# Block one's last 1x1 convolution: half of its tiles made once behind the 3x3 stage and kept, the Gram matrix for the other half only

## The chip, the cores and the metric

The kernel runs on one core of one Trainium2 chip. The metric is device time in microseconds (us) of one execution: TensorE (PE in the profile) with its weight loads (PEld), VectorE (DVE), ScalarE (ACT), GpSimd (POOL), and the DMA engines, which are fed by queues on SyncE (SP), ACT and POOL. A tile framework puts the semaphores between the engines; each engine and each queue works through its own instructions in order. Where an instruction isn't pinned to the order of the program, a scheduler places it on its engine.

## The reference

Two residual blocks, one behind the other, in fp32, on x of 64 images, 1024 channels, 14 x 14 pixels:

```
out = relu(bn(conv(x,   w1, b1, 1, 0), g1, be1))     # 1x1, 1024 -> 256
out = relu(bn(conv(out, w2, b2, 1, 1), g2, be2))     # 3x3,  256 -> 256
out = bn(conv(out, w3, b3, 1, 0), g3, be3)           # 1x1,  256 -> 1024
out = softplus(residual_scale)[0] * out
out = relu(x + out)
```

`bn` takes mean and variance of each channel over all images and pixels (12544 of them) in the call itself. So no convolution's result can be normalized before the convolution has been made, or its statistics have been had in another way, for all images.

## The kernel before

Channels lie on the 128 partitions in slots: 1024 channels are 8 slots (`CS`), 256 are 2 (`MS`). The pixels are cut into T = 32 tiles of two images, 392 pixels (`PX`) each. A tile of x is 128 x 8 x 392 fp32, 1568 KB. The result of conv1 and conv2, `y_all`, stays on the chip; the result of block one, `mids`, goes to DRAM and comes back in block two. PSUM is handled by `Psum`, which gives out banks by tag (ax, ay, ap for conv1; cx, cy, cp for conv3).

The two 1x1 convolutions are made by a scheme of seven products in place of eight half-size ones (`Seven`, with `Conv1` and `Conv3`): sums of the weight blocks (`combine_w1`, `combine_w3`) and of the input blocks (`column_sums` for conv3) are made ahead, products p1 to p7 run on PE, and an `after1` to `after7` behind each product adds it to where it belongs. A conv3 unit makes two slots of output (q and q + 4) of a tile, from 7 matmuls of 196 columns; a tile has four units. A conv1 unit makes a whole tile, by 28 matmuls of 196 columns. `stream` puts the products of neighbouring units into the order in which they are issued.

In `Conv3`, ACT copies three of the products out with the scale of the normalization (line 352, called from `saved`), DVE adds the scaled others into the tile of x in place (line 519), POOL adds ACT's copies (lines 540 and 545), ACT applies shift and relu, and behind the tile's last unit ACT's queue stores the tile to `mids`.

Block one goes: conv1 of all tiles; the 3x3 stage `conv2`; the statistics of conv3; and the stage `fused`. The statistics of conv3's result are not taken from that result. `gram` makes the Gram matrix of conv3's input: y is normalized (ACT, `norm`), a constant is subtracted (DVE, line 1179), chunks of 128 pixels are turned so that pixels lie on partitions, and for each of the 98 chunks PE multiplies the chunk with itself (`cp<-zt` and `ap<-zt` in the profile; the PE array is used there as 128 x 64 tiles). The first pieces are turned by PE (line 1221), the others by pieces moved by DMA (line 1200, queues of SP and POOL) and turned by DVE in 32 x 32 blocks (line 1237). `conv3_stats` (lines 1317 to 1366) makes mean and variance of every output channel from it by a few matmuls with w3. Eight plain conv3 results of tile 0 (`made`) are issued around it, and `affine` turns statistics into scale and shift.

`fused` (line 1422) interleaves two streams one to one: conv3 of tiles 1 to 31 (`last_convs`) with conv1 of block two on tiles 0 to 31 (`first_convs`), the former LAG = 14 products ahead. A tile of x is loaded by SP one tile ahead of its use (`load_x`, one DMA), turns into a tile of block one's output in place, and is then the input of conv1. There are two pools of x tiles with two buffers each, used by even and odd tiles in turn. Block two ends with the same Gram stage and `final`.

Of the kernel before, what the change touches and what calls it, by code (L numbers as in the profile page):

```python
# [14 lines left out]
P = 128  # L43
# [21 lines left out]


# [24 lines left out]
def bottlenecks(ctx: ExitStack, tc: tile.TileContext, x, w1s, w2s, w3s, pars, out):  # L91
# [8 lines left out]
    mids = [dram.tile([P, CS * PX], FP, tag=f"mid{t}", name=f"mid{t}") for t in range(T)]  # L100
    us = [
# [45 lines left out]
    def sums_tile(pool, n):  # L147

        return pool.tile([P, n, 4 * CS // 2 * P], FP, tag="ws", name="ws")

    def combine(a, s):

        s = s.rearrange("p (i s m) -> p i s m", i=4, m=P)
        s = [s[:, i] for i in range(4)]
        def work():
            for to, one, op, two in (
                (s[0], a[1][0], ALU.add, a[1][1]), (s[1], s[0], ALU.subtract, a[0][0]),
                (s[2], a[0][0], ALU.subtract, a[1][0]), (s[3], a[0][1], ALU.subtract, s[1]),
            ):
                tc.keep_in_program_order(nc.vector.tensor_tensor(to, one, two, op))  # L160
                yield

        return (a, s), work()
# [4 lines left out]
    def combine_w3(w, s):  # L168
        n = CS // 2
        return combine([[w[:, k, o * n : (o + 1) * n] for k in range(MS)] for o in range(2)], s)  # L170
# [183 lines left out]
    class Conv1(Seven):  # L354
# [5 lines left out]
        def __init__(self, psum, pool, xs, ts, w1, par, stats, border):  # L360
            self.psum, self.pool, self.ts, self.par, self.stats = psum, pool, ts, par, stats
            self.border = border if ts[-1] == T - 1 else None
            self.pinned = ts[-1] >= T - 1 - len(ts)
# [64 lines left out]
        def result(self, o, i, bank, more=None):  # L428
# [11 lines left out]
            if len(self.ts) == 2 or o != i:  # L440

                self.run(nc.vector.bn_stats(self.stats[:, o, self.ts[i % len(self.ts)], :], whole), o, i)
# [32 lines left out]
    def column_sums(pool, ys, n, twice=(2, 3)):  # L475
# [6 lines left out]
        nc.vector.tensor_sub(t3, ys[1][1], ys[0][1])  # L482
        nc.vector.tensor_add(t2, t3, ys[0][0])
        nc.vector.tensor_sub(t1, ys[0][1], ys[0][0])
        nc.vector.tensor_sub(t4, ys[1][0], t2)
        return sums

    class Conv3(Seven):
# [6 lines left out]
        def __init__(self, psum, pool, xt, q, n, ys, sums, w3, aff, to):  # L495
# [5 lines left out]
            self.u12 = pool.tile([P, 2 * n], FP, tag="cu12", name="cu12", bufs=2)  # L501
# [48 lines left out]
        def end(self):  # L550
            for row in range(2):
                self.relu(row)
            if self.to is not None:
                nc.scalar.dma_start(out=self.to, in_=self.xt.rearrange("p s f -> p (s f)"))

# [576 lines left out]
    def gram(psum, pool, homes, aff, minus_c, beside):  # L1132

        upper, lower = psum.tile(3 * Q + 1, "cp"), psum.tile(2 * Q + 2, "ap")
        zts = [pool.tile([P, CH, M + 2], FP, tag=f"zt{i}", name=f"zt{i}") for i in range(NZT)]
# [4 lines left out]
        def ends(v):  # L1142

            (step, n), (_, _) = v.ap
            return bass.AP(v.tensor, v.offset + 1, [[step, n], [3 * Q, 2], [1, Q + 1]])
# [4 lines left out]
        once, twice = 1.0 / NPX, 2.0 / NPX  # L1150
# [3 lines left out]
        for i, here, cols, value in (  # L1154
# [6 lines left out]
            nc.gpsimd.memset(by[i][here, cols], value)  # L1161

# [71 lines left out]
        def by_vector(k, i):  # L1234
            zt, x = next(zts), home(k)[0].rearrange("p s j f -> p (s j) f")
            tc.keep_in_program_order(
                nc.vector.transpose(
                    zt[:, :, 1 : M + 1].rearrange("p b (n c) -> p b n c", c=32),
                    x[:, :, i * CH * 32 : (i + 1) * CH * 32].rearrange("p n (b r) -> p b n r", r=32),
                )  # L1240
            )
# [55 lines left out]
        for k, zt in enumerate(itertools.chain(pairs(), (None,))):  # L1297
            if before is not None:
                for c in range(CH):
                    first, last = k == 1 and c == 0, k == total and c == CH - 1  # L1300
                    v = before[:, c]
                    for q, with_ in enumerate((v[:, : 3 * Q + 1], v[:, Q + 1 :], v[:, 2 * Q + 1 :], ends(v))):
                        here = slice(q % 2 * Q, q % 2 * Q + Q)
                        to = (upper, lower)[q // 2][here]
                        to = to[:, : 2 * Q + 1] if q == 2 else to
                        if q == 3:
                            to = to.rearrange("p (k m) -> p k m", k=2)
                        matmul(
                            to, v[:, 1 + q * Q : 1 + q * Q + Q], with_, start=first, stop=last,
                            tile_position=(0, q % 2 * Q), skip_group_check=True,  # L1310
                        )
# [5 lines left out]
    def conv3_stats(psum, one, grams, w3, mv, tags, spare):  # L1317
# [10 lines left out]
        turned = psum.tile(P, "ax")  # L1328
# [6 lines left out]
        nc.scalar.activation(g0[high, 0:1], g0[high, M + 1 :], AF.Copy)  # L1335
        means = g0[:, 0:1], g1[:, M + 1 :]
        wide = 64
        sums = [psum.tile(CS * wide, tag).rearrange("p (o k) -> p o k", k=wide) for tag in ("ax", "ap")]
# [8 lines left out]
        for h in range(2):  # L1347
# [3 lines left out]
            matmul(t0, g0[:, left], w3[:, 0, cols, :], start=True, stop=True)  # L1351
            matmul(t1, g0[:, right], w3[:, 0, cols, :], start=True, stop=False)
            matmul(t1, g1[:, right], w3[:, 1, cols, :], start=False, stop=True)
            qs = [q[:, s, h * half * P : (h + 1) * half * P] for s in range(MS)]
            for s, t in ((0, t0), (1, t1)):
                nc.vector.tensor_mul(qs[s], t, w3[:, s, cols, :].rearrange("p o c -> p (o c)"))
            nc.vector.tensor_add(qs[0], qs[0], qs[1])
        for o in range(CS):
            matmul(sums[0][:, o], by_mean[:, o * P : (o + 1) * P], ones, start=True, stop=True)
        for o in range(CS):  # L1360
            matmul(sums[1][:, o], q[:, 0, o * P : (o + 1) * P], ones, start=True, stop=True)
        nc.vector.tensor_copy(mv[:, :, 0], sums[0][:, :, 0])
# [59 lines left out]
    def fused(psum, pool, xpools, xs, w1, w3, aff, par, stats, border, begun):  # L1422

        def last_convs():
            for t in range(1, T):
                if t + 1 < T:
                    xs.append(load_x(xpools[(t + 1) % 2], 0, t + 1))
                ys = [[two(t, s)[:, i * H // 2 : (i + 1) * H // 2] for i in range(2)] for s in range(MS)]  # L1430
                n = PX // 2
                sums = column_sums(pool, ys, n)
                for q in range(CS // 2):
                    yield Conv3(psum, pool, xs[t], q, n, ys, sums, w3, aff, mids[t] if q == CS // 2 - 1 else None)

        def first_convs():
            for t in range(T):
                yield Conv1(psum, pool, xs[t : t + 1], (t,), w1, par, stats, border)

        a, c = stream(first_convs(), T), stream(last_convs(), (T - 1) * CS // 2)  # L1440
# [5 lines left out]
        while True:  # L1446
            more = next(a, "end"), next(c, "end")
            if more == ("end", "end"):
                break

# [202 lines left out]
    for b in range(2):  # L1653
# [9 lines left out]
        with tc.tile_pool(name=f"last_{b}", bufs=1) as one, tc.tile_pool(  # L1663
# [4 lines left out]
            if b == 0:  # L1668
                w1 = load_w1(one, b + 1, nc.sync)
            aff = affine(aggregate(stats2, 0), pb, G2, BE2)  # L1670
            with ExitStack() as scope:
                if b == 0:
                    psum = Psum(scope, ["cy", "ay", "cx", "cy", "ay"], cy=2, ay=2)
                else:
                    psum = Psum(scope, ["cy", "cx"], cy=2, cx=2, cp=2)
                with tc.tile_pool(name=f"gram_{b}", bufs=1) as pool:
                    def x_tile(name, t=0):
                        return xpools[t].tile([P, CS * PX], FP, tag="x", name=name)


                    ws = sums_tile(one, 2 - b)
                    homes = [x_tile("home"), x_tile("home") if b else ws.rearrange("p i n -> p (i n)"), x_tile("home", 1)]

                    made_c, summed = combine_w3(w3, ws[:, 0])
                    weights = [made_c]
                    total = NPX // (CH * P)
                    if b == 0:
                        made_a, more = combine_w1(w1, ws[:, 1])
                        weights = [made_a, made_c]
                        beside = {total - 10: partial(list, summed), total - 4: partial(list, more)}  # L1690
                    else:
                        beside = {total - 14 + 2 * i: partial(next, summed) for i in range(4)}
                    grams = gram(psum, pool, homes, aff, minus_c, beside)

                    made = [conv3(psum, 0, 0, w3, "cx" if b else "ay")]
                    mv3 = small.tile([P, CS, nc.vector.BN_AGGR_DIM], FP, tag="mv3", name="mv3")
                    conv3_stats(psum, pool, grams, w3, mv3, ("cy", "cp", "cy", "cp" if b else "cx"), homes[2])
                made.append(conv3(psum, 0, 1, w3, "cx" if b else "ay"))
                tags = ("cy", "cp") * 2 if b else ("cy", "cx", "cy")
# [59 lines left out]
```

## Time and profile before

| | |
|---|---|
| median of the runs | 1913.37 us (1912.12 to 1913.9, 3 runs) |
| span of the profiled execution | 1910.9 us |
| from the span's start to the end of `conv2` | 0 to 584 us |
| Gram stage | 584 to 645 us |
| conv3's statistics, tile 0, start of `fused` | 645 to 671 us |
| `fused` | 671 to about 1254 us |
| last stage of block two, after its Gram stage | about 1610 to 1911 us |

The page gives the busy time of each engine, the chain of work that ended last, and groups of instructions by line, engine and tile name. A group's row has the count, the busy time, the mean length of one in ns, and the idle time of its engine before it with what ended that. An fp32 matmul shows as two records. The windows view gives, for each stretch, the busy time of every engine, the granted clock of TensorE (1.00 is full), the share of time in which the 16 DMA engines were busy and the bandwidth. The timeline merges neighbouring instructions of one group into one row: start, length, group, count.

### The profile page before, as it was taken

The page shows a single profiled execution, that of the slowest core. Times are in us where ns is not written, and L with a number is a line of the kernel's source. Part 1 is how long each engine was busy: PE and PEld are TensorE (multiplying, and loading weights), DVE is VectorE, ACT ScalarE, POOL GpSimd, SP SyncE. Part 2 cuts the span into 40 slices and gives each one's busy share as a digit, 9 for nine tenths or more (in the row PEclk, how much of TensorE's full clock was granted, in tenths as well). Part 3 has the DMA queues.
Part 4 walks back from the last instruction along what each step waited for, and adds up shares of the span by engine and source line. Part 5 has one row for each costly group of instructions (what it writes and reads, how often), then busy time and mean ns, then how long its engine had stood idle before and what let it go on. Part 6 is the DMA issues. An engine that isn't in the chain of part 4 may idle for free. (4 is left out here: it accounts for less than half of the span.)

```text
span 1910.9 us, 28713 instructions
## 1 busy us (share of the span) xinstructions
PE 1899.0 (99%) x10232; PEld 1594.9 (83%) x10232; DVE 1541.5 (81%) x2491; ACT 1085.6 (57%) x2160; POOL 581.6 (30%) x682
## 2 busy tenths in 40 slices
PE   9999999999999999999999999999999999999999
PEld 5555557999998799999999999989999987555555
DVE  5787767999998867776777777689999986888886
ACT  2222214677778355555555555557777782666665
POOL 0111100211204143333334333302121051666665
PEclk9999999999999999999999999999999999999999
DMA  7777644887856544444444444258779467799997
GB/s 288 273 248 271 219 166 144 208 224 213 215 171 172 190 158 176 170 169 169 174 185 176 175 169 169 111 191 216 217 206 226 143 166 274 263 349 334 354 342 274
DMA packets 198527, 408.77 MB, mean 214 GB/s; under 512 B 37104, under 2 KB 175024, under 8 KB 181872
## 3 DMA queue, kind: packets, MB, share of 16 engines
q1 hardware_dynamic: 159712, 321.85, 49.3%
q0 software_dynamic: 33056, 34.03, 8.6%
q10 hardware_dynamic: 5616, 51.06, 6.4%
q8 instruction: 81, 1.33, 0.3%
q14 instruction: 62, 0.51, 0.1%
HBM read 263.75 MB, written 115.34 MB: 198 GB/s over the span
## 5 line engine op out<-in xcount | busy, mean ns | idle before, releaser
L352 ACT ACTIVATE cu<-cy,scale 128x196 f32<-128x196 f32 (+1 forms) x552 | 256.2, 473 | 275.2 <-PE cy L179 272.6
L179 PE MATMUL columns<-v,ub 128*128 128x224 f32 (+1 forms) x1536 | 302.3, 338 | 1.1 <-ACT columns L352 0.8
L352 ACT ACTIVATE x<-x,shift 128x392 f32<-128x392 f32 x452 | 255.2, 613 | 73.1 <-POOL x L545 53.6
L179 PEld LDWEIGHTS columns<-v,ub 128*128 128x128 f32 x1536 | 268.8, 188 | 6.7 <-ACT columns L352 1.5
L519 DVE SCALAR_TENSOR_TENSOR x<-cp,scale,x 128x196 f32<-128x196 f32 (+1 forms) x368 | 178.1, 484 | 95.3 <-PE cp L179 94.1
L179 PE MATMUL cy<-ct,ws 128*128 128x196 f32 (+1 forms) x736 | 221.6, 383 | 0.7 <-ACT cu L352 0.7
L540 POOL TENSOR_TENSOR x<-x,cu 128x196 f32<-128x196 f32 (+1 forms) x184 | 165.6, 900 | 172.9 <-ACT cu L352 164.2
L179 PE MATMUL ay<-at,ws 128*128 128x196 f32 (+1 forms) x768 | 212.8, 382 | 0.0
L545 POOL TENSOR_TENSOR x<-x,cu 128x392 f32<-128x392 f32 x124 | 125.9, 1016 | 191.4 <-DVE x L519 191.4
L179 PEld LDWEIGHTS ay<-at,ws 128*128 128x128 f32 x768 | 139.3, 190 | 34.7 <-issue 0.2
L179 PEld LDWEIGHTS cy<-ct,ws 128*128 128x128 f32 x736 | 133.6, 190 | 35.3 <-ACT cu L352 2.6
L179 PE MATMUL l<-diffs,ub 128*128 128x224 f32 (+1 forms) x768 | 149.6, 337 | 0.3 <-ACT sd L1492 0.3
L567 POOL TENSOR_TENSOR x<-x,cu 128x392 f32<-128x392 f32 x120 | 125.5, 1047 | 73.2 <-DVE x L519 72.3
L179 PE MATMUL m<-sums,ua 128*128 128x224 f32 (+1 forms) x752 | 146.0, 336 | 0.2 <-DVE sums L683 0.2
L352 ACT ACTIVATE au<-ay 128x196 f32<-128x196 f32 (+1 forms) x140 | 53.4, 381 | 150.2 <-PE ay L179 142.7
L179 PEld LDWEIGHTS l<-diffs,ub 128*128 128x128 f32 x768 | 134.6, 189 | 1.2 <-ACT sd L1492 0.6
L519 DVE SCALAR_TENSOR_TENSOR x<-cx,scale,x 128x196 f32<-128x196 f32 (+1 forms) x184 | 88.9, 483 | 57.0 <-PE cx L179 57.0
L179 PEld LDWEIGHTS m<-sums,ua 128*128 128x128 f32 x752 | 131.5, 189 | 1.3 <-DVE sums L683 0.7
L179 PE MATMUL cy<-y,w 128*128 128x196 f32 (+1 forms) x408 | 125.1, 393 | 0.0
L179 PE MATMUL cx<-y,w 128*128 128x196 f32 (+1 forms) x400 | 122.7, 392 | 0.0
L179 PE MATMUL cp<-y,ws 128*128 128x196 f32 (+1 forms) x368 | 112.1, 386 | 0.0
L179 PE MATMUL cy<-ct,w 128*128 128x196 f32 (+1 forms) x368 | 111.1, 384 | 0.6 <-ACT cu L352 0.5
(237 smaller groups left out, 3903.7 us busy)
## 6 DMA issues: line engine op xcount, KB each, us to landing
x<-in_x SPq DMA_DIRECT2D x62, 1568.0 KB, 7.0
ub<-u SPq DMA_DIRECT2D x92, 768.0 KB, 5.6
x<-mid SPq DMA_DIRECT2D x32, 1568.0 KB, 8.8
mid<-x ACTq DMA_DIRECT2D x31, 1568.0 KB, 5.1
out<-x SPq DMA_DIRECT2D x123, 392.0 KB, 6.8
ua<-u SPq DMA_DIRECT2D x92, 256.0 KB, 3.1
u<-y POOLq DMA_DIRECT2D x48, 256.0 KB, 5.8
home<-y SPq DMA_DIRECT2D x70, 96.0 KB, 3.5
```

The lines of the kernel that those rows point to most:

```text
L179: tc.keep_in_program_order(nc.tensor.matmul(*args, **kw))
L352: tc.keep_in_program_order(nc.scalar.activation(*args, **kw))
L519: nc.vector.scalar_tensor_tensor(v, bank, self.scale[:, o : o + 1], v, ALU.mult, ALU.add)
L540: nc.gpsimd.tensor_add(self.part(1, 1), self.part(1, 1), u3)
L545: nc.gpsimd.tensor_add(v, v, self.u12)
L567: nc.gpsimd.tensor_add(v, v, self.u12[:, i * self.n : (i + 1) * self.n])
```

## The change

In block one, tiles 16 to 31 (`KEPT = 16`) get their conv3 in a new stage, `mixed`, right behind conv2 and before the statistics are known. The new unit `Direct` is a conv3 unit without scale, residual or relu. Its results go into an SBUF buffer `kept`, by ACT's copies, DVE's adds and POOL's add; DVE takes `bn_stats` of both output slots, and SP stores them to DRAM tiles `zs`. Between the products of these 64 units stand the Gram products of the other 49 chunks (tiles 0 to 15): one from unit 8 on behind product 3 of each unit, a second one in every fourth unit from unit 20 on. All 49 are turned by DVE, from pieces that DMAs move; no chunk is turned by PE. `conv3_stats` is now a generator, one step of which is issued at a time behind the last chunks. The statistics of conv3 come from aggregating sixteen `bn_stats` entries and two that are made from the Gram result. Within the stage, normalization is done tile by tile (ACT), and the subtraction and column sums go to POOL; the sums of w3 are made by POOL too.

`fused` now goes over 32 positions: even position p is tile p/2, with conv3 as before; odd position p is tile 16 + p//2, whose conv3 result is read back. Conv3's products are issued at half the rate (one for two of conv1). For odd positions `kept_rows` fetches each of the tile's eight rows of z (128 x 392, 200 KB) by SP into one of two beds (space of the raw weights w1 and w3, no longer needed), adds it scaled to the tile of x (even rows by one DVE instruction; odd rows by two POOL instructions), applies shift and relu by ACT, and fetches the row after next. Behind the eighth row ACT's queue stores the tile. x is loaded three positions ahead, in four DMAs a tile.

```diff
+KEPT = T // 2
+NGRAM = KEPT * PX
+MOVES = 5 * P * CH, 5 * P * CH, 5 * P * CH, 5 * P * CH, 9 * P
+BEGIN, FASTER = 8, 20
...
+    class Direct(Conv3):
...
+        def part(self, row, i):
+            return self.z[:, row, i * self.n : (i + 1) * self.n]
+
+        def saved(self, v, row):
+            act(v, self.y, AF.Copy)
+            return v
+
+        def after2(self):
+            nc.vector.tensor_add(self.part(0, 0), self.x, self.u12[:, : self.n])
+
+        def after5(self):
+            act(self.part(1, 1), self.p, AF.Copy)
+
+        def after3(self):
+            nc.vector.tensor_add(self.part(0, 1), self.p, self.u12[:, self.n :])
+
+        def after4(self):
+            act(self.part(1, 0), self.y, AF.Copy)
+
+        def end(self):
+            for row in range(2):
+                nc.vector.bn_stats(self.stats[:, self.o[row], self.t - KEPT, :], self.z[:, row])
+            to = zs[self.t - KEPT].rearrange("p (s f) -> p s f", s=CS)[:, self.q :: CS // 2, :]
+            tc.keep_in_program_order(nc.sync.dma_start(out=to, in_=self.z))
...
+    def mixed(psum, pool, one, x_right, x_left, aff, minus_c, w3, made_c, summed_a, mv3):
...
+        homes = [x_right.tile([P, CS * PX], FP, tag="x", name="home") for _ in range(2)]
+        kept = [x_left.tile([P, CS // 2, 2, PX], FP, tag="x", name="kept") for _ in range(2)]
...
+        def prepare(t):
+
+            for s in range(MS):
+                norm(s, two(t, s), aff, act)
+                less(two(t, s), s, nc.gpsimd)
+                yield
+            ready[t] = column_sums(pool, blocks(t), n, range(4), nc.gpsimd)
+            yield
...
+        for k, _ in enumerate(stream(units(), total, together=True)):
+            unit, step = divmod(k, 7)
...
+            if unit >= BEGIN and (step == 2 or (step == 5 and q == 3 and unit >= FASTER)):
+                if next(grams, "end") == "end":
+                    if tail is None:
+                        tail = conv3_stats(
+                            psum, pool, (upper, lower, by, gs), w3, mv3,
+                            ("ay", "ay", "ap", "ax"), homes[1], ("ay", "ay", "ay"),
+                        )
+                    next(tail, None)
...
+    def fused(psum, pool, one, xpools, xs, raw, w1, w3, aff, par, stats, border, begun):
...
+        places = [KEPT * (p % 2) + p // 2 for p in range(T)]
...
         def last_convs():
-            for t in range(1, T):
-                if t + 1 < T:
-                    xs.append(load_x(xpools[(t + 1) % 2], 0, t + 1))
+            for p in range(2, T, 2):
+                t = places[p]
...
+        def kept_rows():
+
+            rows = [(p, o) for p in range(1, T, 2) for o in range(CS)]
+
+            def bring(r):
+                if r < len(rows):
+                    p, o = rows[r]
+                    nc.sync.dma_start(out=beds[r % 2], in_=zs[places[p] - KEPT][:, o * PX : (o + 1) * PX])
+
+            bring(0)
+            bring(1)
+            for r, (p, o) in enumerate(rows):
+                v = xs[p][:, o, :]
+                if o % 2:
+                    nc.gpsimd.tensor_scalar(beds[r % 2], beds[r % 2], scale[:, o : o + 1], None, ALU.mult)
+                    nc.gpsimd.tensor_add(v, v, beds[r % 2])
+                else:
+                    nc.vector.scalar_tensor_tensor(v, beds[r % 2], scale[:, o : o + 1], v, ALU.mult, ALU.add)
+                act(v, v, AF.Relu, bias=shift[:, o : o + 1])
+                bring(r + 2)
+                if o == CS - 1:
+                    nc.scalar.dma_start(out=mids[places[p]], in_=xs[p].rearrange("p s f -> p (s f)"))
+                yield
...
+        a, c, rows = stream(first_convs(), T), stream(last_convs(), (KEPT - 1) * CS // 2), kept_rows()
+        done = LAG
         for i in range(LAG):
             next(c)
...
-        while True:
-            more = next(a, "end"), next(c, "end")
-            if more == ("end", "end"):
+            if i % 3 == 2:
+                next(rows)
+        for k in itertools.count():
+            p, step = divmod(k, 28)
+            if step == 6 and p + 3 < T:
+                assert len(xs) == p + 3
+                xs.append(load_x(xpools[(p + 3) % 2], 0, places[p + 3], 4))
+            if k % 7 == 3:
+                next(rows, None)
+            if next(a, "end") == "end":
                 break
+            while done < LAG // 2 + (k + 1) // 2:
+                next(c, None)
+                done += 1
```

More of the change, by code (lines that the diff above doesn't have):

```diff
@@ L100, in bottlenecks @@
     mids = [dram.tile([P, CS * PX], FP, tag=f"mid{t}", name=f"mid{t}") for t in range(T)]
+    zs = [dram.tile([P, CS * PX], FP, tag=f"z{t}", name=f"z{t}") for t in range(KEPT, T)]
     us = [
@@ L1234, in by_vector @@
         def by_vector(k, i):
[L1235 to L1241, printed above, removed]
+            zt = next(zts)
+            turn(zt, home(k)[0], i * CH)
             return zt
@@ L1300, in gram @@
                     first, last = k == 1 and c == 0, k == total and c == CH - 1
[L1301 to L1311, printed above, removed]
+                    gram_products(upper, lower, before[:, c], first, last)
             before = zt
@@ L1320, in conv3_stats @@
+    def conv3_stats(psum, one, grams, w3, mv, tags, spare, single=("ax", "ax", "ap")):
         upper, lower, by, (g0, g1) = grams
```

267 lines of the change are left out of this document (212 added, 55 removed).

## The prediction

> **What bounds the kernel now.** I read the first part of the page, then the windows stage by stage, then the TensorE (PE) timeline at the seams, then the groups of the fused stage and the DMA issues.
>
> ```profile
> span 1910.9 us, 28713 instructions
> PE 1899.0 (99%) x10232; PEld 1594.9 (83%) x10232; DVE 1541.5 (81%) x2491; ACT 1085.6 (57%) x2160; POOL 581.6 (30%) x682
> ```
> ```profile
> core 0: us, PE busy (x) PEld busy (x) DVE busy (x) ACT busy (x) POOL busy (x), PEclk, DMA share, GB/s
> 584.00:646.00 62.00, 61.49 (x825) 53.34 (x824) 53.94 (x87) 44.99 (x44) 23.39 (x38) 1.00 0.74 218
> 700.00:800.00 100.00, 100.00 (x605) 100.00 (x604) 70.94 (x156) 54.13 (x128) 37.55 (x43) 1.00 0.45 176
> 1100.00:1200.00 100.00, 100.00 (x605) 100.00 (x604) 70.51 (x159) 55.13 (x129) 39.16 (x44) 1.00 0.46 177
> 1700.00:1800.00 100.00, 100.00 (x301) 56.58 (x300) 83.52 (x128) 67.47 (x128) 69.07 (x65) 1.00 0.97 341
> ```
> PE is busy 99% of the span at a full granted clock, so the end moves by what PE work disappears and by what idle time appears. The profiled span of 1910.9 us stands 2.5 us below the median of the runs, 1913.37; I do the sum on the span and add 2.5. In the fused stage PE has 605 records in 100 us, two for each matmul: 0.331 us for a matmul of 196 columns, so a tile of 56 (28 of conv1, 28 of conv3) takes 18.5 us, with DVE busy 71% and the DMA engines 45%. What the change works with is mostly spare, except PE.
>
> **What is removed: half of the Gram stage, less the switches it brings.** The Gram stage by the PE timeline (start, length, group):
>
> ```profile
> 584.58 0.60 PE L1221 MATMUL cy<-ident,y 128*128 128x128 f32 x4
> ...
> 588.32 0.66 PE L1221 MATMUL cx<-ident,y 128*128 128x128 f32 x4
> 588.90 0.55 PE L179 MATMUL cp<-zt 128*64 128x193 f32 x4
> ...
> 590.15 0.66 PE L1221 MATMUL cy<-ident,y 128*128 128x128 f32 x4
> ...
> 599.78 0.49 PE L179 MATMUL cp<-zt 128*64 128x193 f32 x4
> 600.10 0.39 PE L179 MATMUL ap<-zt 128*64 128x129 f32 x4
> 600.33 0.49 PE L179 MATMUL cp<-zt 128*64 128x193 f32 x4
> ...
> 645.40 1.58 PE L179 MATMUL ay<-y,w 128*128 128x392 f32 x4
> 646.82 0.27 PE L1329 MATMUL ax<-ident,g 128*128 128x128 f32 x1
> ...
> 655.84 1.54 PE L179 MATMUL ay<-y,w 128*128 128x392 f32 x4
> ```
> The stage runs from 584.58 to 645.40: 60.8 us for 98 chunks of 128 pixels. Undisturbed, a chunk costs 600.33 − 599.78 = 0.55 us. A pair of chunks with four transposes costs 590.15 − 588.32 = 1.83 us. A transpose of 128 columns is about 0.331/2 × 128/196 = 0.108 us, so the pair should take 2 × 0.55 + 4 × 0.108 = 1.53 us: the other 0.30 us are its two turns between PE tiles of 128x128 (transposes) and 128x64 (Gram). In the stage before there are few such turns. After the change every one of the 49 remaining chunks stands alone between conv3 matmuls of 128x128, so each pays two turns: 0.85 us, and I take 0.87, since a full 196-column matmul that follows has more to refill than a transpose. 49 × 0.87 = 42.6 us, and the stage's saving is 60.8 − 42.6 = 18.2 us. Bounds: 60.8 − 49 × 0.55 = 33.8 us if the turn is free, and 60.8 − 49 × 1.15 = 4.4 us if it costs twice the 0.30. The Trainium skill, "TensorEngine Tiling (Array Packing)", Key Properties, speaks against the change at this place: a change of the tiling mode drains TensorE, while a change of the tile within a mode does not. The row agrees (0.30 us for two turns); without that rule the sum below would be 15.6 us lower.
>
> The statistics' own matmuls (646.82 to 655.84, 9.0 us) are the same after; they are only spread between the last units. The conv3 matmuls are the same too: 8 whole ones of tile 0, and 124 units of 7 × 4 half-tile products, 64 of them now ahead of the statistics and 60 in the fused stage. The conv1 matmuls stay.
>
> **What is added in the mixed stage.** Groups of the fused stage (700 to 1200 us) and of the stretch from 560 to 680 us: busy, mean ns | idle before:
>
> ```profile
> L352 ACT ACTIVATE x<-x,shift 128x392 f32<-128x392 f32 x216 | 123.1, 614 | 45.2 <-POOL x L545 45.2
> L545 POOL TENSOR_TENSOR x<-x,cu 128x392 f32<-128x392 f32 x108 | 109.7, 1016 | 169.7 <-DVE x L519 169.7
> L519 DVE SCALAR_TENSOR_TENSOR x<-cp,scale,x 128x196 f32<-128x196 f32 x216 | 90.0, 417 | 58.9 <-PE cp L179 58.9
> L442 DVE BATCH_NORM_STATS2 stats<-y 128x6 f32<-128x392 f32 x54 | 30.2, 559 | 0.0
> L352 ACT ACTIVATE au<-ay 128x196 f32<-128x196 f32 x81 | 26.5, 327 | 13.8 <-PE ay L179 13.8
> L470 DVE TENSOR_TENSOR at<-x,at 128x784 f32<-128x784 f32 x27 | 26.3, 975 | 33.4 <-PE ay L179 33.4
> ```
> ```profile
> L352 ACT ACTIVATE y<-y,shift,scale 128x1536 f32<-128x1536 f32 x12 | 19.2, 1659 | 0.1
> L1237 DVE STREAM_TRANSPOSE zt<-home 128x512 f32<-128x512 f32 x29 | 18.6, 684 | 1.2 <-PE ap L179 0.9 <-DMA ws<-y 0.3
> ```
> (The group L352 of 128x1536 is the normalization of y, 1.08 ns per column.) A unit of the mixed stage is 7 matmuls, 2.32 us on PE. ACT empties five of its banks by plain copies, 5 × 0.327 = 1.64 us, and normalizes: two slots of the next tile, 2 × 392 columns, over four units (0.21 us a unit) and a Gram piece's share of up to 0.75 us. That is up to 2.6 us, so the eight units without a Gram chunk run about 0.28 us late each: +2.2. From the ninth unit on the chunk lengthens the unit to 2.32 + 0.87 = 3.19 us, which covers ACT. DVE has two statistics (2 × 0.56), two short adds (2 × 0.42) and a transpose of 0.68 for every two chunks, together 2.3 us: also covered. The stores (400 KB a unit, 126 GB/s) leave room below the 341 GB/s of the final stage. At the start the first unit waits for the affine of conv2's statistics, then one normalization, one subtraction and the column sums, with conv3's weight sums now made on POOL: I put 2 us there, bounds 0 and 5. The end of the stage is covered by the eight conv3 of tile 0 (8 × 1.32 = 10.5 us by the row at 655.84 and its likes) against some 6 us of aggregation and affine.
>
> **What is moved in the fused stage: the weak point.** A pair of tiles now takes 56 conv1 matmuls and 28 of conv3: 84 × 0.331 = 27.8 us on PE. DVE has per pair 2 × 3.9 (column sums of conv1), its evictions, and four new rows of 0.62 to 0.7 us: 21 to 23 us; ACT and POOL have less. So on paper PE still bounds it, and the fused stage would lose nothing. But each kept tile needs its eight rows of z (200 KB each) fetched, scaled and added in turn, through only two beds, and the fetches stand on SP's queue between the loads of x. SP's order in the changed kernel repeats by pair: four parts of x for the even position, four parts for the odd one, rows 2 to 7 of the odd one's z, rows 0 and 1 of the next z, then the next even position's x. SP works in that order, and each row's fetch waits until its bed has been read: by DVE for even rows, by POOL for odd ones.
>
> ```profile
> x<-in_x SPq DMA_DIRECT2D x62, 1568.0 KB, 7.0
> out<-x SPq DMA_DIRECT2D x123, 392.0 KB, 6.8
> ua<-u SPq DMA_DIRECT2D x92, 256.0 KB, 3.1
> home<-y SPq DMA_DIRECT2D x70, 96.0 KB, 3.5
> ```
> ```profile
> x<-in_x SPq DMA_DIRECT2D x27, 1568.0 KB, 6.5
> ```
> (The second is the fused stage alone.) A z row of 200 KB lies between 96 KB (3.5 us) and 256 KB (3.1 us): I take 3.1, bounds 2.5 and 4. POOL takes two instructions for an odd row: the add is L545's 1.02 us; a scaling of 392 columns is not in the trace, between 0.5 (half of an add) and 1.02; I take 0.9 and 0.1 for the signals, so 2.0 us, and a hop (fetch and POOL) is 5.1 us. The Trainium skill, "GPSIMD Engine Reference", Engine selection, has one-input elementwise work at roughly line rate and two-input work at half of that; by it the scaling would be an estimate of 0.5 us and the hop 4.7; no run here shows that scaling.
>
> The loop, from the moment t when conv1 has released a buffer and the odd position's x is issued: first part landed t + 3.5; row 1 through POOL t + 5.5; row 3 fetched behind the other three parts of x (whole load 6.5 to 7) t + 8.6, through POOL t + 10.6; row 5 t + 15.7; row 7 t + 20.8; then rows 0 and 1 of the next z are issued, and only then the next even position's x, t + 21.3. Its third part, which holds the second output row of conv3's first unit, lands 5 us later (three quarters of 6.5), t + 26.3. That unit's DVE eviction frees PE's next bank (0.5 us), and the conv1 products that read the old buffer end 2.2 us after it: t + 29.0 is the next t. PE wants it at t + 27.8. So by these values PE waits 1.2 us a pair. The loop breaks even at a hop of 4.7 us, since it has three. The DMA load speaks for longer: a pair moves two loads of x and two stores (4 × 1.6 MB) and z (1.6 MB), 8 MB in 27.8 us, 288 GB/s, against 177 before; at 341 GB/s a 392 KB transfer is among those of 6.8 us median. With hops of 5.4 the loop is 29.9. I take 2.0 us a pair, 14 pairs: 28 us, bounds 0 and 5 a pair. The first kept tile has its eight rows behind three loads of x and 16 to 20 us until conv1 needs it, against a chain of 20 us or more: +4, bounds 0 and 8.
>
> **The sum.** −18.2 (Gram) + 2 (start) + 2.2 (eight units) + 4 (first kept tile) + 28 (row loop) = +18.0: span 1928.9, runs 1931.4 us. I forecast 1931, that is slower.
>
> **Rivals.**
> - Faster, the chain is hidden: a hop of 4.7 us or less, so that PE never waits for x in the fused stage. −18.2 + 2 + 2.2 + 3 = −11 us: 1902. For it: 392 KB parts and single rows are smaller than any load before, and the threshold is only 0.4 us away. Against: the DMA load rises by 60%.
> - Much faster, the turns are free as well: −33.8 + 6 = −28: 1885. For it only that PE may preload across a turn; against it 1.83 us where 1.53 would be due.
> - Slower by more, the DMA engines are the bound of the row chain: with a row at 4 us and a part of x at 7, a hop is 6 us and the loop 27.8 + 4.5: 14 × 4.5 = 63 us, −18.2 + 8 + 63 = +53: 1966. It decides from a hop of 6 us on. For it 6.8 us for 392 KB in the final stage, where the DMA share is 0.97; against it that here it would be some 0.75.
> - Slower, in the mixed stage: PE waits for banks that ACT empties in order. The start of the fused stage has this at one unit alone, 670.64 − 667.97 = 2.67 us for 2.32:
>
> ```profile
> 667.97 0.49 PE L179 MATMUL cy<-y,w 128*128 128x196 f32 x2
> ...
> 670.64 0.50 PE L179 MATMUL cy<-y,w 128*128 128x196 f32 x2
> ```
>  64 × 0.35 = 22 us; with the row chain hidden that is −11 + 22 − 2 = +9: 1922. Against it: the plain copy is 0.1 us shorter than the scaled one there, and the Gram chunk lies between.
>
> **How the numbers follow.** My forecast 0.42 (its own range 1917 to 1950), chain hidden 0.23, turns free as well 0.06, DMA bound 0.16, mixed stage 0.07, and 0.06 that a loop loss of 0.8 us a pair just cancels the gain (−11 + 11: 1913). The range of 8 in 10 leaves out the free turns and the upper half of the DMA case: 1896 to 1964. About 0.2% (3.8 us) is what a measurement of this kernel can tell from no change. Faster by more: 0.23 + 0.06 and a part of the cancelling case, 0.31; within: 0.06; slower: 0.63.
>
> **What would show it.** In the PE timeline of the mixed stage: a Gram chunk between two units that takes 0.85 to 0.9 us (0.55 would be free turns), and units of 2.3 us without one. In the windows of the fused stage: PE busy 93 to 95% where it is 100% now, its idle time put down to DVE's evictions of x or to the load of x, once per pair; a period of 29 to 30.5 us from one even position's x to the next; SP's fetches of z ending one after another 4.7 to 5.5 us apart for odd rows. PE at 100% there would make the forecast wrong towards faster; a busy DMA of over 0.9 in that stage with rows landing after 4 us towards slower. Idle PE in the mixed stage over 8 us would make its part wrong.

## The result, and the profile after

The changed kernel takes 2070.2 us (median of 4 runs, 2069.55 to 2070.45) against 1913.63 us: ratio 1.082, 95% interval 1.080 to 1.083. It is slower, as forecast, but by 157 us and not by 18. First the page of the changed kernel, then its windows by stage (up to conv2's end, the fused stage, block two behind it) and two stretches within:

```profile
span 2067.8 us, 28976 instructions
PE 1947.9 (94%) x9802; PEld 1596.0 (77%) x9802; DVE 1576.0 (76%) x2466; ACT 1105.2 (53%) x2295; POOL 732.3 (35%) x809
```
```profile
core 0: us, PE busy (x) PEld busy (x) DVE busy (x) ACT busy (x) POOL busy (x), PEclk, DMA share, GB/s
600.00:700.00 100.00, 92.89 (x590) 74.90 (x588) 62.00 (x134) 63.73 (x168) 59.94 (x78) 0.98 0.48 153
1000.00:1100.00 100.00, 82.05 (x439) 78.46 (x438) 59.98 (x112) 41.15 (x93) 45.85 (x43) 0.90 0.61 216
...
0.00:584.00 584.00, 581.15 (x2472) 444.49 (x2472) 486.27 (x622) 270.87 (x536) 74.34 (x116) 1.00 0.70 219
840.10:1410.60 570.50, 483.52 (x2607) 463.50 (x2605) 348.52 (x658) 243.29 (x548) 263.25 (x243) 0.92 0.60 212
1410.60:2067.80 657.20, 650.27 (x3333) 499.75 (x3333) 575.09 (x815) 445.12 (x821) 262.83 (x280) 1.00 0.79 255
```

In the fused stage no engine is full: PE is busy 85%, DVE 61%, the DMA engines 60%, and PE has 439 records in 100 us where it had 605. That is what a chain of waits looks like. The granted clock, 1.00 everywhere before, is 0.92 there. The span by stages, with the 64 moved conv3 units (64 x 7 x 0.331 = 148.3 us) counted on the side where they now are:

| | before | after | difference |
|---|---|---|---|
| to the end of conv2 | 584.3 | 583.8 | −0.5 |
| from there to the first conv1 product of the fused stage | 87.1 + 148.3 = 235.4 | 256.3 | +20.9 |
| fused stage | 581.4 − 148.3 = 433.1 | 570.4 | +137.3 |
| block two behind it | 658.1 | 657.2 | −0.9 |

The start times of PE's 2605 records in the fused stage split its loss: in 71 places PE's next record comes over 0.36 us after the last, together 101 us more than due; 199 records follow each other at 0.27 to 0.36 us instead of 0.166, together 32 us; smaller delays make 6 us. The kernel before has no such places: its windows of 100 us in the prediction hold 605 records each.

Where PE stands still in a pair of tiles, and what the row chain does meanwhile (timelines of the changed kernel: rows of PE, where 0.86 us for two records instead of 0.49 means half speed, then SP's and POOL's):

```profile
1015.08 1.02 PE L157 MATMUL cy<-ct,w 128*128 128x196 f32 x2 [3.91 <-ACT cu L330]
1042.84 1.07 PE L157 MATMUL ay<-at,ws 128*128 128x196 f32 x4 [3.04 <-DVE at L431]
1043.71 0.86 PE L157 MATMUL cx<-y,w 128*128 128x196 f32 x2
...
1052.15 0.60 PE L157 MATMUL cy<-ct,w 128*128 128x196 f32 x2 [1.72 <-ACT cu L330]
```
```profile
1025.61 1.76 SPq L107 DMA_DIRECT2D x<-in_x  x4
1030.53 0.89 SPq L1636 DMA_DIRECT2D w<-z  x2
...
1049.87 0.32 SPq L1636 DMA_DIRECT2D w<-z  x1
1050.29 1.79 SPq L107 DMA_DIRECT2D x<-in_x  x4
...
1061.94 1.76 SPq L107 DMA_DIRECT2D x<-in_x  x4
```
```profile
1029.07 1.02 POOL L1644 TENSOR_TENSOR x<-x,w 128x392 f32<-128x392 f32 x1 [2.62 <-DMA x<-in_x]
...
1035.07 1.26 POOL L1643 TENSOR_SCALAR w<-w,scale 128x392 f32<-128x392 f32 x1 [2.66 <-DMA w<-z]
1036.41 1.52 POOL L1644 TENSOR_TENSOR x<-x,w 128x392 f32<-128x392 f32 x1
1041.66 2.18 POOL L1643 TENSOR_SCALAR w<-w,scale 128x392 f32<-128x392 f32 x1 [3.73 <-DMA w<-z]
1043.92 1.01 POOL L1644 TENSOR_TENSOR x<-x,w 128x392 f32<-128x392 f32 x1
...
1047.48 1.26 POOL L1643 TENSOR_SCALAR w<-w,scale 128x392 f32<-128x392 f32 x1 [1.25 <-DMA w<-z]
1048.83 1.01 POOL L1644 TENSOR_TENSOR x<-x,w 128x392 f32<-128x392 f32 x1
```

The first half of the prediction's loop is there, step by step: the odd position's x is issued at 1025.61, row 1 is added at 1029.07, rows 3, 5 and 7 come through POOL one after another until 1049.84, then follow the next z row (1049.87) and the next even position's x (1050.29); at 1061.94 the next odd x. That is 24.7 + 11.6 = 36.3 us, where the prediction had 21.3 + 7.7 = 29.0. Eleven such rounds of this stage took 36.9 us on average.

The second half runs another way. The prediction had PE wait for the even position's x. But PE goes on at 1052.15, and the first part of that x, issued at 1050.29, lands only at 1053.59. What PE waited for is a copy on ACT, ACT waited for an addition of a conv3 unit on POOL (L519), and that addition stood behind row 7 in POOL's order. In the same way the 3.04 us before 1042.84 are a column sum of conv1 on DVE (L431), which stood behind row 4 while its fetch was on the way:

```profile
1049.80 0.60 POOL L519 TENSOR_TENSOR x<-x,cu 128x196 f32<-128x196 f32 x1
1050.43 0.62 ACT L330 ACTIVATE x<-x,shift 128x392 f32<-128x392 f32 x1 [3.55 <-POOL x L519]
1051.68 0.73 ACT L330 ACTIVATE cu<-cy,scale 128x196 f32<-128x196 f32 x2
```
```profile
1041.28 0.62 DVE L1646 SCALAR_TENSOR_TENSOR x<-w,scale,x 128x392 f32<-128x392 f32 x1 [4.22 <-DMA w<-z]
1041.82 0.97 DVE L431 TENSOR_TENSOR at<-at,x 128x784 f32<-128x784 f32 x1
```

So the rows hold PE up by standing ahead of other work in the order of POOL, DVE and ACT. Nothing needs them yet: conv1's first column sum on this tile runs at 1067.9, 18 us after row 7's addition, and 18 to 20 us after it in every round looked at.

### The profile page after: what moved, and what is told of

The parts are those of the page before. It is cut to its first block, busy times and chain, and to the rows that moved or that the text cites. A ratio compares the mean times of both kernels' runs of the same rounds, so it can differ in the third digit from the quotient of the medians.

```text
span 2067.8 us, 28976 instructions
## 1 busy us (share of the span) xinstructions
PE 1947.9 (94%) x9802; PEld 1596.0 (77%) x9802; DVE 1576.0 (76%) x2466; ACT 1105.2 (53%) x2295; POOL 732.3 (35%) x809
## 3 DMA queue, kind: packets, MB, share of 16 engines
q8 instruction: 78, 1.28, 0.2%
## 5 line engine op out<-in xcount | busy, mean ns | idle before, releaser
L330 ACT ACTIVATE cu<-cy,scale 128x196 f32<-128x196 f32 (+1 forms) x360 | 177.6, 502 | 216.0 <-PE cy L157 214.2
L157 PEld LDWEIGHTS ay<-at,ws 128*128 128x128 f32 x768 | 152.0, 209 | 43.5 <-DVE at L431 7.0
L498 DVE SCALAR_TENSOR_TENSOR x<-cp,scale,x 128x196 f32<-128x196 f32 (+1 forms) x240 | 124.4, 518 | 52.2 <-PE cp L157 50.9
L579 POOL TENSOR_TENSOR x<-x,cu 128x392 f32<-128x392 f32 x120 | 125.5, 1047 | 73.3 <-DVE x L498 71.1
L519 POOL TENSOR_TENSOR x<-x,cu 128x196 f32<-128x196 f32 (+1 forms) x120 | 114.0, 950 | 74.4 <-ACT cu L330 62.4
L1643 POOL TENSOR_SCALAR w<-w,scale 128x392 f32<-128x392 f32 x64 | 84.9, 1326 | 152.8 <-DMA w<-z 152.8
L157 PE MATMUL cy<-ct,wt 128*128 128x196 f32 x496 | 129.7, 345 | 7.1 <-ACT cu L330 6.4
L157 PEld LDWEIGHTS cy<-ct,w 128*128 128x128 f32 x368 | 65.8, 198 | 79.1 <-ACT cu L330 58.6
L330 ACT ACTIVATE y<-y,shift,scale 128x1568 f32<-128x1568 f32 (+7 forms) x102 | 119.4, 1183 | 8.7 <-DVE shift L1749 8.6
L993 POOL DMA_DIRECT2D y<-f x24 | 32.3, 1643 | 236.3 <-DVE f L913 236.3
```

Of the source, the lines that this page charges most:

```text
L157: tc.keep_in_program_order(nc.tensor.matmul(*args, **kw))
L330: tc.keep_in_program_order(nc.scalar.activation(*args, **kw))
L498: nc.vector.scalar_tensor_tensor(v, bank, self.scale[:, o : o + 1], v, ALU.mult, ALU.add)
L519: nc.gpsimd.tensor_add(self.part(1, 1), self.part(1, 1), u3)
L579: nc.gpsimd.tensor_add(v, v, self.u12[:, i * self.n : (i + 1) * self.n])
L993: nc.gpsimd.dma_start(out=out_rows[3][:, o], in_=fa[:, o, :full], accum_op=ALU.add)
```

## The experiments

The theories on the fused stage: (1) SP's order, with the even x queued behind eight rows; (2) full DMA engines; (3) loads of x that are late by themselves; (4) POOL's two instructions as the pace; (5) the chain of rows through two beds, written down after e1 to e4. Each run is one time (beside 1912.4 to 1913.6 us for the kernel before) with a profile; "a pair" is the median time of two tiles in the fused stage, from ACT's `y<-ay` instructions (after: 36.7 us, before with the moved units: 37.1, without them 27.8).

**The ceiling (e1), the fetches on ACT (e2), all rows on DVE (e3), both (e4).**

```diff
e1 -  bring(0); bring(1); bring(r + 2); both adds of a row
e2 -  nc.sync.dma_start(out=beds[r % 2], ...)
e2 +  tc.keep_in_program_order(nc.scalar.dma_start(out=beds[r % 2], ...))
e3 -  if o % 2: nc.gpsimd.tensor_scalar(...); nc.gpsimd.tensor_add(...)
e3    nc.vector.scalar_tensor_tensor(v, beds[r % 2], scale[:, o : o + 1], v, ...)
```

> The kept rows are neither fetched nor added (the odd tiles go on without their conv3 part; relu, store and loads of x stay). Theory 1 (SP's order: the fetches of z stand between two loads of x, and each waits for its bed): with no fetch on SP a pair of tiles falls from 36.5 us to 28 to 29 us, and the whole to 1930 to 1950 us. Theory 2 (the DMA engines are full): z is 20% of the fused stage's traffic, so the period falls to about 32 us, 1990 to 2010 us. Theory 3 (loads of x, three positions ahead and gated by conv1's release of the buffer, are late on their own): no change beyond 20 us.

> The same fetches, issued by ACT right behind the relu that follows the row's add, so that SP has only loads of x. Theory 1: the loads of x go out as soon as conv1 releases a buffer, a pair takes 28 to 30 us, 1935 to 1970 us. Theory 2 (full DMA engines): the same bytes, so 2050 us or more. Theory 4 (POOL's two instructions for a row, 1.3 and 1.2 us, set the pace): nothing changes for POOL, 2040 us or more.

> All eight rows are added by DVE in one instruction (0.6 to 0.8 us) instead of every second one by POOL in two (2.6 us); fetches stay on SP. Theory 1: the row chain on SP gets shorter by three to four times 1.5 us, so a pair takes 31 to 33 us and the whole 1990 to 2020 us. Theory 4 (POOL sets the pace): 28 to 29 us a pair, 1940 to 1960 us. Theory 2: no change.

> Fetches on ACT and all rows on DVE. Theory 1: little beyond e2, 1930 to 1965 us. Theory 4: the gain comes only here and in e3, with e2 at 2040 us or more. Theory 2: 2030 us or more.

Measured: e1 1938.7 us, a pair 28.5; e2 2060.5, 35.9; e3 2000.3, 31.4; e4 2015.5, 33.0. Without row work (e1) the loads of x, three positions ahead, cost next to nothing: the fused stage takes 442.3 us, 9 more than due, and the clock is back at 1.00. So theory 3 falls, and 128 of the 137 us hang on the rows. e3 fits theory 1 and theory 5 alike (a shorter hop); for theory 4 it should have come to 1940 to 1960. e2 contradicts theory 1: SP carries only x there and the pair hardly moves. It is where theories 2 and 4 had it. POOL's waits in e2, from 870 to 1250 us:

```profile
POOL w L1643 <- DMA w<-z: 115.7, 41, 5.9
```

That is no less than in the change (104.4 us in the same stretch): the rows come no sooner, since a fetch now waits on ACT for the relu of the row two before, and takes 4.2 us to land instead of 2.9. And e4 is slower than e3, outside theory 1's range. Theory 2 falls with e1, e3 and e4: with rows on DVE (e3) the stage moves 246 to 259 GB/s, more than the change, and is faster. Theory 4 is still open here.

**Eight beds (e5), and three more parts.** y of the last four tiles is idle until late in the fused stage; its space holds eight beds for the first twelve kept tiles.

```diff
e5 +  wide = [y_all[:, s, NPX - (i + 1) * PX : NPX - i * PX] for s in range(MS) for i in range(4)]
e5 +  bed(r): wide[r % 8] for the first 96 rows, then beds[r % 2]; bring(r + 8) behind row r
e6 +  two chunks at every second place (GROUP = 2)
e7 +  load_x of positions 0, 2, 1 at units 59, 61, 62 of mixed
```

> For the first twelve kept tiles the rows of z are fetched into eight beds (space of y that the last four tiles' conv1 results fill later) instead of two; rows, engines and SP as in the change, the last four kept tiles as before. Theory 5 (the row chain itself sets the pace: each fetch waits until the bed's last row has been added, and rows stand in program order on ACT, DVE and POOL, on whichever queue the fetch is): with a tile's eight rows fetched ahead a pair takes 29 to 31 us in the first twelve, whole 1970 to 2000 us. Theory 1 (SP's order alone: the even position's x is still queued behind all eight rows): 33 us or more a pair, 2030 us or more. Theory 4 (POOL's two instructions for a row): 2040 us or more, since POOL does the same.

> Two Gram chunks at every second place instead of one at every place: 24 pairs of turns between the PE tile shapes fewer. By the trace a lone chunk costs 0.90 us where 0.55 is due, so theory (turns cost 0.35 us a pair) expects 24 x 0.35 = 8.4 us less, 2058 to 2065 us, and 1.45 us for a place with two chunks. Rival (the lost time there is ACT and DVE being late for the units, which the chunk merely covers): no change in the mixed stage, 2068 to 2072 us.

> The loads of x for positions 0, 2 and 1 are issued during the last five units of the mixed stage, as their buffers come free, instead of behind its last store. Theory (PE's 11 to 12 idle us at the start of the fused stage come from these late loads): 8 to 12 us less, 2058 to 2063 us. Rival (the wait is for the rows of the first kept tile, which stand on ACT before conv3's copies): under 5 us less, 2065 us or more.

> Eight beds, chunks by two and early x together: the sum of the three by their theories, 1950 to 1985 us.

Measured: e5 1994.6 us, a pair 29.8 in the first twelve tiles, and 35 to 37 in the last four, which still have two beds. POOL's work, SP's order and the bytes are as in the change; only the fetch has left the chain. That is theory 5, and it speaks against theory 4. The windows from 1000 to 1100 us of e1, e3 and e5, beside 82.05 for PE and a clock of 0.90 in the change:

```profile
1000.00:1100.00 100.00, 98.53 (x589) 97.33 (x588) 72.02 (x134) 56.31 (x126) 22.51 (x29) 1.00 0.59 226
1000.00:1100.00 100.00, 91.33 (x514) 87.42 (x513) 75.02 (x142) 49.02 (x111) 22.66 (x24) 0.97 0.68 247
1000.00:1100.00 100.00, 95.67 (x567) 93.56 (x567) 80.83 (x143) 52.59 (x120) 64.94 (x58) 1.00 0.77 275
```

e6: 2067.0 us, between the two theories; a place with two chunks takes 1.45 us, as expected, but from conv2's end to the first conv1 product it is only 3.7 us shorter instead of 8.4. Where the rest is lost was not followed up. e7: 2068.1 us; the first conv1 product starts 0.7 us earlier, so the rival holds. With x there in time, PE stands 4.85 us for ACT's copy, which is queued behind a kept row's relu:

```profile
832.63 0.62 ACT L330 ACTIVATE x<-x,shift 128x392 f32<-128x392 f32 x1 [4.51 <-POOL x L1647]
833.16 0.41 ACT L330 ACTIVATE cu<-cy,scale 128x196 f32<-128x196 f32 x1
```

e8: 1984.3 us, just inside its range, and the first conv1 product at 828.3 instead of 840.1: with eight beds the early x counts too.

**The relu one row later (e9 to e11), and a filler for PE (e12).**

```diff
e9  -  act(v, v, AF.Relu, bias=shift[:, o : o + 1])        # of row r
e9  +  of row r - 1, except that a tile's last row is not put off
e12 -  busy(psum, "m", 7)
e12 +  busy(psum, "m", 19 if b == 0 else 7)
```

> The change, with each kept row's relu on ACT issued one row later (3.5 us of PE work further on), but for a tile's last one; beds, fetches and adds as in the change. Theory 5a (PE stands still because ACT waits in order for a row's add, ahead of the copies that free conv3's and conv1's banks): a pair falls from 36.7 to 31 to 33 us, 1985 to 2015 us. Theory 5b (the chain of fetch and add over two beds sets the pace by itself, wherever the relu stands): 35 us or more, 2045 us or more.

> The same on top of the eight beds of e5. Theory 5a: 28.5 to 29 us a pair in the first twelve (e5: 29.8), 1978 to 1985 us. Theory 5b: as e5, 1990 to 1996 us.

> e8 (eight beds, chunks by two, early x) with the late relu. Theory 5a: 10 to 15 us below e8, 1968 to 1975 us. Theory 5b: as e8, 1982 to 1986 us.

> The change with 12 more of the dummy matmuls that keep PE busy behind conv2 (4.7 us), while the first tile of the mixed stage is normalized. In the trace of the change PE's matmuls take 0.65 us instead of 0.33 for some 4.5 us after this idle stretch. Theory (the slow matmuls follow from PE's idleness): the first seven products take 2.3 us instead of 4.6, total 2 to 3 us less. Rival (they are slow for another reason, such as the first use of the weights or of the banks): the same 4.6 us, total unchanged or longer by the filler's overhang.

Measured: e9 2076.5 us (a pair 37.2), e10 2002.4, e11 1988.6: nothing won, 4 to 8 us lost. e9 is within 5b's range; e10 and e11 lie above the ranges of both theories. ACT's order is where the wait shows, not what makes it. From 870 to 1250 us ACT waits 98.9 us for POOL's additions of the conv3 units in e9 and 98.6 us in the change; they stand on POOL behind a kept row's, wherever that row's relu stands. e12: 2073.9 us, 4 longer and not 2 to 3 shorter. The filler (14.5 us with the old one) ended late, at 593.96, but the first products behind it run at full speed:

```profile
593.96 0.82 PE L157 MATMUL cy<-y,w 128*128 128x196 f32 x4
594.62 0.49 PE L157 MATMUL cx<-y,w 128*128 128x196 f32 x2
```

In the change the same products, behind 4.78 us of idleness, take twice as long:

```profile
588.57 1.68 PE L157 MATMUL cy<-y,w 128*128 128x196 f32 x4 [4.78 <-DVE y L1360]
590.04 0.86 PE L157 MATMUL cx<-y,w 128*128 128x196 f32 x2
```

So the slow matmuls follow from idleness: weights and banks are the same in both.

**SP in the program's order (e13, e14), and eight beds with all rows on DVE (e15, e16).**

```diff
e13 +  tc.keep_in_program_order(...) around every bring and every load_x of the fused stage
e14    e13 with e3's rows;  e15  e5 with e3's rows;  e16  e15 with e6 and e7
```

> The fetches of z and the loads of x stand on SP in the program's order: the even position's x four rows earlier than in the change, the odd one's behind row 5 of the tile before; beds, engines and row work as in the change. Theory 1 (the loop closes over the even position's x, queued behind all eight rows): a pair falls to 29 to 32 us, 1950 to 2000 us. Theory 5b (the rows' chain over two beds, in POOL's and DVE's order, sets the pace wherever x stands): 34 us or more, 2030 us or more.

> The same with all rows on DVE. Theory 1: as e13 or 1 us a pair below it. Theory 5b: a hop of fetch and add is 3.8 instead of 5 us, so as e3 (31.4 us a pair), 1990 to 2005 us.

> Eight beds for the first twelve tiles and all rows on DVE. Theory 5b: with rows fetched ahead neither POOL's pair nor the fetch is in a chain: 28.5 to 29.3 us a pair in the first twelve (e1 without rows: 28.5), 31.4 in the last four, 1965 to 1980 us. Rival (DVE, then at 78 to 80% busy, becomes late for PE's banks): 30 us or more a pair, 1985 us or more.

> e15 with chunks by two and early x: 10 to 15 us below e15, 1952 to 1968 us; still above the kernel before, since without any rows the change stands at 1938.7 us.

Measured: e13 2088.7 us (a pair 37.1), e14 2045.3 (35.5), e15 1958.6 (28.9 in the first twelve), e16 1949.0. e13 is above every number that theory 1 gave, and within 5b's: moving x forward on SP only exchanges what waits. SP's waits in e13 (us in total, times, longest):

```profile
SPq L1637 <- POOL x L1646: 183.0, 23, 10.0
SPq L107 <- PE ap L157: 139.0, 23, 10.2
```

Now rows wait behind an x that waits for PE, as before x waited behind rows that wait for POOL. e14 misses theory 5b's own number (1990 to 2005). SP stands at loads of x for 186 us there, and a row takes 5.5 us to land instead of e3's 3.1: the fetch is late although the work on a row is short. So SP's order is a price too, when the program's order makes it worse; it is not the one that the change pays most for. e15 confirms the chain: with neither fetch nor POOL in it, a pair is 0.4 us from the e1 without rows, and DVE, 83% busy, is not late, against the rival; it came out 6 us below the expected range, and e16 3 us below its own. e16 is still 36 us above the kernel before, and e1, which leaves the rows out, 25 above: none of these beats it.

## Why the prediction was wrong

- **Direction and place: right, the direction partly by luck.** PE bounds the kernel before; the weak point is the kept rows in the fused stage, and the first rival (chain hidden) did not come. But that rival had the kernel 11 us faster without row waits, and e1, without any row work, is 25 us slower: the mixed stage alone would have made the direction come true, against the sum's terms for it.
- **The row loop, the step that failed.** The prediction put 2.0 us a pair, with bounds 0 and 5, 28 us in all; it is 36.3 − 27.8 = 8.5 us a pair, and the stage lost 137. The chain of rows was right, with terms that were too small. The way from the last row back to conv1 was wrong: it does not lead over the even position's x.
  - "A hop (fetch and POOL) is 5.1 us": rows 3 and 5 took 7.0 each and row 7 4.9, by the times above (1030.96 is the second fetch of the pair at 1030.53; 1037.93, 1044.93 and 1049.84 the ends of the adds). Over twelve kept tiles they took 6.8, 7.4 and 5.0 us on average, 19.1 for the three hops instead of 15.3. POOL's part is 8.2 us of that instead of 6.0: the scaling, bounded by 0.5 and 1.02 us, takes 1.33, and the add 1.25 instead of 1.02. The fetch was well priced as a median of all rows (2.9 us against 3.1), but not in the chain: rows 3, 5 and 7 took 3.3, 4.8 and 2.5 us to land.

```profile
L1643 POOL TENSOR_SCALAR w<-w,scale 128x392 f32<-128x392 f32 x47 | 62.4, 1327 | 115.4 <-DMA w<-z 115.4
L1644 POOL TENSOR_TENSOR x<-x,w 128x392 f32<-128x392 f32 x47 | 58.7, 1248 | 34.9 <-PE cy L157 17.7 <-DMA x<-in_x 14.3
...
w<-z SPq DMA_DIRECT2D x94, 196.0 KB, 2.9
```

  The bound from a two-input add was no upper bound for a one-input scaling. What makes row 5's fetch late was not tried.
  - "That unit's DVE eviction frees PE's next bank (0.5 us), and the conv1 products that read the old buffer end 2.2 us after it", with 5 us for x to land before: 11.6 us from the even x to the next odd one, instead of 7.7. PE did not wait on that way, as the times above show. In the waits from 820 to 1350 us no addition of conv3 into a tile (L498) waits for a load of x. PE's largest are for ACT's copies and for DVE's evictions:

```profile
PE cy L157 <- ACT cu L330: 52.0, 16, 6.0
PE cp L157 <- DVE x L498: 14.9, 13, 2.1
DVE x L498 <- PE cy L157: 61.2, 14, 6.5
```

  PE is held by the rows until 1052.15, and then 16 of conv1's 28 matmuls on the old buffer are still ahead; with conv3's between them they end when the next odd x is issued, 1061.94.
  - Idle time was priced as idle time only. Behind long waits the matmuls run at half speed (32 us in the stage by PE's start times; how much of it lengthens the loop was not tried).
- **That SP closes the loop** is not what the trace shows, and e2 and e13, in which the even x no longer stands behind eight rows, win 9.7 us and lose 18.5. They also bring another price in: in both, row 7's addition comes 3 to 5 us after conv1's first column sum on the same tile, where the change has it 18 to 20 us before. So the rows hold up conv1 of the odd tile itself there. How much each way would cost alone was not separated.
- **Gram and its turns: right.** The prediction had 0.87 us for a lone chunk; it is 0.90 by the starts (0.79 longer to the next product, which takes 0.105 more to its second record), 49 x 0.90 = 44.1 us, a saving of 16.7 us against 18.2. The timeline of one:

```profile
621.21 0.55 PE L157 MATMUL ap<-zt 128*64 128x193 f32 x4
621.59 0.39 PE L157 MATMUL ax<-zt 128*64 128x129 f32 x4
621.91 0.60 PE L157 MATMUL cp<-ct,wt 128*128 128x196 f32 x2
622.35 0.49 PE L157 MATMUL cy<-ct,wt 128*128 128x196 f32 x2
```

- **The mixed stage: too cheap.** The sum had 8.2 us up to the first conv1 product; the table's 20.9 and the 16.7 saved make 37.6. For its start 2 us were put; PE idles 4.78 us and then loses 2.2 at half speed. For the units without a chunk 2.2; up to the first chunk PE takes 29.3 us for 59 products (19.5 due), 7.5 more than the half speed explains. For the first kept tile 4; the 14 conv3 products before the first conv1 take 16.7 us instead of 4.6. The rest, 13 us, is lost between the first chunk and the last unit, 195.0 us for 128.8 of products, 44.1 of chunks and 9.0 of statistics. The rival of the mixed stage had 22 us; so it came true in size, together with the forecast's own case and not instead of it. Its cause is not shown: behind the start PE's listed waits in this stage are 4.5 us for DVE's turned chunks, 2.5 for DVE's adds and 1.2 for ACT's copies.
- **The rival of full DMA engines** fell as to its cause: the DMA share is 0.60, and the median z row landed in 2.9 us, not 4. The average hop of 6.4 us is above the 6 at which it was to decide all the same.

The Trainium skill, "TensorE: Matmul & The Clock Gate", Part 1: The HAM clock gate, says that PE falls to half its clock after about 3.4 us of idleness and needs about as much busy time to return. This case agrees on the return, since the half clock lasts 3.4, 6.8 or 10.2 us in the fused stage; the idleness that it takes is less here (the last section has the numbers). The prediction didn't draw on it; at its own 2 us a pair no wait would have come near 3.4 us. On the Trainium skill's "GPSIMD Engine Reference", Engine selection, which the prediction quoted for 0.5 us, the measurement decides: 1.33 us.

## What to carry to other kernels

A chain of fetch, work and release through few buffers is priced by its whole round, with its longest measured hop and what else stands on each engine in it; if that round is near the time that it must fit into, more buffers are worth more than any reordering (two beds to eight won 76 us, moving queues 10 at best). Where every engine works in order, a late side stream holds up what stands behind it, even when its own result is not needed for another 18 us. It costs three times: the wait, the work that could not run beside it, and the half-speed clock behind it. Before saving matmuls on a PE that is 99% busy, ask whether the data that comes back will always be early.

## What the hardware showed unexpectedly

A one-input scaling by a per-partition value on POOL (392 columns, fp32) took 1.26 us undisturbed and 1.28 to 1.44 on average in the runs that have it, longer than a two-input add of the same size (1.02 us undisturbed). How long PE may idle at full clock is not a matter of the single wait's length. Two waits at the start of the fused stage:

```profile
826.35 0.60 PE L157 MATMUL cy<-y,w 128*128 128x196 f32 x2 [2.79 <-DVE x L1559]
826.78 0.49 PE L157 MATMUL cx<-y,w 128*128 128x196 f32 x2
...
834.55 1.02 PE L157 MATMUL cy<-ct,wt 128*128 128x196 f32 x2 [6.04 <-ACT cu L330]
835.37 0.86 PE L157 MATMUL cy<-y,w 128*128 128x196 f32 x2
```

2.79 us left the matmuls at full speed, 6.04 us did not. But 2.66 us before 906.10 did not either, and in e13 3.72 us before 1012.33 did. The traces' records of the granted clock show why: in all 18 traces the clock changes only at steps of 3.41 us. A step at full clock in which PE stood idle for over 2.0 us, by its busy times, was followed by a step at half clock each time, one with under 1.4 us never. So two waits of the same length can end differently: one may fall into a single step, the other over two. In this kernel one more turn of the PE tile shape costs some 0.35 us a pair (1.45 us for two chunks together, 2 x 0.90 alone).
